# Conditioned attention with Strassen-Winograd products on one Trainium2 core: scale and shift formed for half of the channels at a time

## The chip, the cores and the metric

The kernel runs on one core of a Trainium2 (trn2) chip. The metric is the device time of one execution in microseconds (us), here the median of three executions.

## The reference

All arrays are float32. `x` is 4 x 1024 x 1024 (batch, token, channel), `cond` is 4 x 1024. Cut to what is computed:

```python
# attention part, 16 heads of 64
scale, shift = split(cond @ W_emb + b_emb, 2)          # W_emb: 1024 x 2048
xn  = rms_norm(x, g_norm) * (1 + scale) + shift        # per batch and channel
q, k, v = split(xn @ W_qkv)                            # W_qkv: 1024 x 3072
q, k = rms_norm(q, g_q), rms_norm(k, g_k)              # per head
o   = softmax(q k^T / 8) v
x   = x + o + o @ W_out
# depthwise causal convolution whose four taps are the four rows of cond
x   = x + conv(x, taps=cond) + b
```

No token can be multiplied with W_qkv before the scale and the shift of its channels are known, and these need a product with all of W_emb (8.4 MB).

## The kernel before

**The work.** For each batch and each of four pairs of head blocks (a `Double`, 16 in all, L530) the product `xn @ W_qkv` is made by Strassen and Winograd's scheme: tokens and channels are split in two, A11 being tokens 0 to 511 with channels 0 to 511, A12 the same tokens with channels 512 to 1023, A21 and A22 the later tokens. Seven products P1 to P7 of blocks or sums of blocks (S1 to S4 on the token side, T1 to T4 on the weight side) are made for four tiles of 128 tokens each: 28 pieces (`piece`, L580, matmuls at L589), each of four accumulated float32 matmuls over k = 0 to 3. P1 is A11 with the plain weights, P2 is A12 with the plain weights, P6 is S2 with T2, P7 is S3 with T3, P4 is A22 with T4, P5 is S1 with T1 and P3 is S4 with plain weights. A piece is evacuated from one of the three PSUM buffers of `ps_m` by ScalarE (P1, L599) or by VectorE (L601 to L610).

**Forming the sums.** `Chunk` (L257) makes, for one k and one half q of the token tiles, the blocks A and the sums S: four 128 x 128 transposes for the channel half c = 0 (`xtp`, L305), their evacuation with scale and shift (`modulate`, L250: ScalarE at L255, VectorE at L253), the same for c = 1, then four sums on VectorE (L321), and a store to the HBM scratch `scrA` (L329), from which later pieces load their operand `a` (L566). `direct` (L568) makes only A11 or A12 of the first tokens, without a trip through HBM (`xtd`, L574). `Weights` (L479) loads blocks of W_qkv (L495), forms T1 to T4 (L510, on GpSimd for the first Double, otherwise on VectorE) and stores them in `scrB` (L511); `load_w` (L540) fetches a piece's weights (plain ones at L547, T ones at L550, three buffers).

**The order.** The instruction order of all engines is written by hand: a planner's clock (`tick`) advances by the cost of each piece, steps are deferred by so many us of that clock, and `need` pulls a step forward. All loads and stores are issued in order by SyncE's queue (SP), which also waits there for the engines; the semaphores of its DMAs are used in turn, eight at a time, so a DMA waits for the eighth before it.

**The start of batch 0**, which the change rewrites, goes as follows.
1. Eight loads of W_emb for the scale (512 KB each, L369), then the first 512 tokens of x (eight loads of 256 KB, L351), then eight loads of W_emb for the shift. For each load two matmuls (L373) with the four columns of `condT` as the stationary operand and 512 columns of W_emb streaming; the result has four rows.
2. Each half is copied to SBUF (L149 by ScalarE, L151 by VectorE), sixteen small transposes (L380) bring scale and shift to the channel-per-partition layout, and L384 and L390 add bias and gain.
3. The weights of P1, the other 512 tokens (L344), the weights of P2, and the four `Weights` of the first Double are loaded. `direct(0, 0)` and `direct(1, 0)` make A11 and A12 of the first 256 tokens.
4. The loop over T runs the pieces in the order of FIRST_PRODUCTS (L521): P1 and P2 of tiles 0 and 1, P1 and P2 of tiles 2 and 3, then P6, P7, P4 for tiles 0, 1 and again for tiles 2, 3, then P5 and P3. Between the first of them stand the other two `direct` calls, the scaling of the second half of the tokens (squares at L222, scaling at L359) and the sixteen groups of chunk transposes.
5. The four `Weights` share two buffers of the tag `ob`; the third and the fourth load only after the first two are stored.

After the 28 pieces comes the loop over the 64 units (`Unit`, L618): scores (L629), softmax, values (L692), with the pieces of the next Doubles, the output products and the convolution put between them.

Of the kernel before, what the change touches and what calls it, by code (L numbers as in the profile page):

```python
# [10 lines left out]
F32 = mybir.dt.float32  # L11
AF = mybir.ActivationFunctionType
ALU = mybir.AluOpType
# [8 lines left out]
def kernel(  # L22
# [153 lines left out]
    nc.vector.tensor_copy(cols, cols_ps[:, :NR])  # L176

    condT = apool.tile([P, HN], F32, tag="rec", name="condT", bufs=1)
    condT = condT[:, : NJ * B].rearrange("p (j b) -> p j b", b=B)
    nc.vector.tensor_copy(condT, cols[:, R_COND:R_G].rearrange("p (b j) -> p j b", j=NJ))  # L180


    gqk = const.tile([P, 1], F32, name="gqk")
# [73 lines left out]
    class Chunk:  # L257
# [31 lines left out]
        def transposes(self, c):  # L289
            b, k, q = self.b, self.k, self.q  # L290
            need("xg", self.name)
            if c == 0:
                if len(combining) == 2:
                    d, *at = combining.pop(0)
                    need(*(("r", d, *at) if d else ("s", *at)))
                combining.append((b, q, k))
                tag, n, bufs = R_HOMES.get((q, k), R_HOME) if b == 0 else R_HOME
                rs = [
                    apool.tile([P, n, QN], F32, tag=tag, name=f"r_{self.name}_{i}", bufs=bufs) for i in range(0, 8, n)
                ]  # L300
                self.r = lambda i: rs[i // n][:, i % n, :]
                self.stores = [(rs[i // n][:, : min(n, 7 - i), :], i, min(i + n, 7)) for i in range(0, 7, n)]
            tp = ps_m.tile([P, 2, QN], F32, tag="m", name=f"xtp_{self.name}_{c}")
            for i in range(4):
                nc.tensor.transpose(tp[:, i // 2, i % 2 * P : (i % 2 + 1) * P], self.source(c, i), ident)  # L305
            tick(0.45)
            for h in range(2):
                place = ((A11, A21), (A12, A22))[c][h]
                modulate(self.r(place), tp[:, h, :], b, k + c * KH, b == 0 and c == 1)
            if c == 1:  # L310
                defer_quiet(1.2, ("s", q, k) if b == 0 else ("r", b, q, k), self.combine)

        def combine(self):
            r = self.r
            for place, (p0, p1, op) in {
                S1: (A21, A22, ALU.add),
                S2: (S1, A11, ALU.subtract),
                S3: (A11, A21, ALU.subtract),
                S4: (A12, S2, ALU.subtract),
            }.items():  # L320
                nc.vector.tensor_tensor(r(place), r(p0), r(p1), op)  # L321
            if (self.b, self.q) == (0, 0):
                defer(STORE, ("r", 0, 0, self.k), self.store)
            else:
                self.store()
# [3 lines left out]
                nc.sync.dma_start(scrA[self.b][self.q][:, i0:i1, self.k, :], src)  # L329


    mod_sb = []
    x0 = {}
    homes = [("qT00", 1), ("kT00", 1), ("qT01", 1), ("kT01", 1), ("v10", 2), ("v10", 2), ("v11", 2), ("v11", 2)]

    def first_tokens(h):
# [3 lines left out]
        for i, t in enumerate(tiles):  # L340
# [4 lines left out]
            else:  # L345
                x0[t] = []
                for g in range(2):
# [2 lines left out]
                    x0[t].append(xt)  # L350
                    nc.sync.dma_start(xt, x[0, t * P : (t + 1) * P, g * HN : (g + 1) * HN])  # L351

        def scale():
            for i, t in enumerate(tiles):
                norm.squares_of(i, x0[t])
            norm.root()
            for t in tiles:
                for g in range(2):
                    nc.vector.tensor_scalar_mul(x0[t][g], x0[t][g], rn[0, t])  # L359

        return scale

    for g in range(2):
        mod_ps = ps_s.tile([P, 2, HN], F32, tag="s", name=f"mod_ps_{g}")
        for k in range(NJ):
            if (g, k) == (1, 0):
                first_tokens(0)()
            we = apool.tile([P, 2, HN], F32, tag="sp", name=f"we_{g}_{k}", bufs=9)
            nc.sync.dma_start(  # L369
                we, w_emb[k * P : (k + 1) * P, g * DIM : (g + 1) * DIM].rearrange("p (h d) -> p h d", h=2)  # L370
            )
            for h in range(2):
                nc.tensor.matmul(  # L373
                    mod_ps[:B, h, :], condT[:, k, :], we[:, h, :], start=(k == 0), stop=(k == NJ - 1)
                )
        mod_sb.append(apool.tile([P, DIM], F32, tag=("mx", "sum")[g], name=f"mod_sb_{g}", bufs=1))
        evacuate(mod_sb[g][:B, :], mod_ps[:B].rearrange("p h d -> p (h d)"))
    modT_ps = ps_m.tile([P, 512], F32, tag="m", name="modT_ps")[:, : 2 * NJ * B]
    for c in range(2 * NJ):
        nc.tensor.transpose(  # L380
            modT_ps[:, c * B : (c + 1) * B], mod_sb[c // NJ][:B, c % NJ * P : (c % NJ + 1) * P], ident[:B, :B]
        )
    mod = const.tile([P, 2 * NJ, B], F32, name="mod")
    nc.vector.tensor_add(  # L384
        mod,
        modT_ps.rearrange("p (c b) -> p c b", b=B),
        cols[:, R_BE:R_GQ].unsqueeze(2).to_broadcast([P, 2 * NJ, B]),
    )
    gain = mod[:, :NJ, :]
    nc.vector.scalar_tensor_tensor(  # L390
        gain,
        mod[:, :NJ, :],
        1.0,
        cols[:, R_G:R_CB].unsqueeze(2).to_broadcast([P, NJ, B]),
        ALU.add,
        ALU.mult,
    )


    class Pair:  # L400
# [73 lines left out]
    def w_block(kh, c, k=None):  # L474

        rows = slice(kh * HN, (kh + 1) * HN) if k is None else slice(kh * HN + k * P, kh * HN + (k + 1) * P)
        return [w_qkv[rows, s * DIM + c * P : s * DIM + (c + 1) * P] for s in range(3)]

    class Weights:  # L479

# [5 lines left out]
        def load(self):  # L486
            d, k = self.d, self.k
            self.b = {}
            four = apool.tile([P, 4, HN], F32, tag="ob", name=f"b_{self.name}", bufs=2)
            for kh in range(2):  # L490
                for y in range(2):
                    t = four[:, 2 * kh + y, :]
                    self.b[kh, y] = t[:, :W3]
                    for s, src in enumerate(w_block(kh, 2 * d + y, k)):
                        nc.sync.dma_start(t[:, s * P : (s + 1) * P], src)  # L495
            if d:
                if d > 1 or k > 1:
                    defer_gap(5.0, ("B", d), 2.5, self.combine)
# [19 lines left out]
        PRODUCTS += [(name, a, t) for t in range(HT)]  # L518
    NPR = len(PRODUCTS)

    FIRST_PRODUCTS = PRODUCTS[:8]  # L521
    for ts in ((0, 1), (2, 3)):
        FIRST_PRODUCTS += [(name, a, t) for name, a in (("P6", S2), ("P7", S3), ("P4", A22)) for t in ts]
    FIRST_PRODUCTS += PRODUCTS[20:]
# [5 lines left out]
    class Double:  # L530
# [9 lines left out]
        def load_w(self, name):  # L540
# [2 lines left out]
            self.w[name] = w  # L543
            block = {"P1": (0, 2 * d), "P2": (1, 2 * d), "P3": (1, 2 * d + 1)}.get(name)
            if block:
                for s, src in enumerate(w_block(*block)):
                    nc.sync.dma_start(w[:, :, s * P : (s + 1) * P], src.rearrange("(k p) d -> p k d", p=P))  # L547
            else:
                need("B", d)
                nc.sync.dma_start(w, scrB[d][:, {"P6": T2, "P5": T1, "P7": T3, "P4": T4}[name]])  # L550
# [669 lines left out]
        return cut(pieces[:n], SHARES) + [pieces[n:]]  # L1220


    doubles[0] = Double(0)
    doubles[0].load_w("P1")
    scale = first_tokens(1)
    doubles[0].load_w("P2")
    for k in range(KH):
        weights[k] = Weights(0, k)
        weights[k].load()
    for s in range(2 * KH):  # L1230
        chunks[0, s] = Chunk(0, s % KH, s // KH)
    doubles[0].direct(0, 0)
    doubles[0].direct(1, 0)
    for k in range(KH):
        weights[k].combine()
    for T in range(NPR):
        if T in (1, 2):
            doubles[0].direct(T - 1, 1)
        if T == 1:
            scale()  # L1240
        if 2 <= T < 2 + KH:
            for s in range(2 * T - 4, 2 * T - 2):
                for c in range(2):
                    chunks[0, s].transposes(c)
        run(piece(T))

    own = []
# [85 lines left out]
```

## Time and profile before

| what | value |
|---|---|
| median of three executions | 2879.78 us (2879.61 to 2885.32) |
| the profiled execution: its own time | 2883.05 us |
| the profiled execution: its span | 2881.0 us |
| TensorE (PE) busy | 2790.8 us, 97% of the span |
| VectorE (DVE) / ScalarE (ACT) / GpSimd (POOL) busy | 76% / 58% / 47% |
| granted TensorE clock, mean | 0.991 |
| DMA | 510.98 MB, mean 177 GB/s |
| first piece (P1 of tile 0) begins | 42.24 us |
| first scores of the first unit begin | 146.20 us |

Times in the profile count from the start of the span. PEclk is the share of its full clock that TensorE was granted. A float32 matmul leaves two records, so a piece of four matmuls is "x8" in a timeline. "Idle before" is followed by what ended the idle time. DMA shares near 1.0 mean that the sixteen DMA engines had no spare time. SPq rows are DMA issues in SyncE's queue.

### The profile page before, as it was taken

The page shows a single profiled execution, that of the slowest core. Times are in us where ns is not written, and L with a number is a line of the kernel's source. Part 1 is how long each engine was busy: PE and PEld are TensorE (multiplying, and loading weights), DVE is VectorE, ACT ScalarE, POOL GpSimd, SP SyncE. Part 2 cuts the span into 40 slices and gives each one's busy share as a digit, 9 for nine tenths or more (in the row PEclk, how much of TensorE's full clock was granted, in tenths as well). Part 3 has the DMA queues.
Part 4 walks back from the last instruction along what each step waited for, and adds up shares of the span by engine and source line. Part 5 has one row for each costly group of instructions (what it writes and reads, how often), then busy time and mean ns, then how long its engine had stood idle before and what let it go on. Part 6 is the DMA issues. An engine that isn't in the chain of part 4 may idle for free.

```text
span 2881.0 us, 32179 instructions
## 1 busy us (share of the span) xinstructions
PE 2790.8 (97%) x10529; PEld 1315.6 (46%) x10529; DVE 2184.3 (76%) x2652; ACT 1684.7 (58%) x2269; POOL 1348.2 (47%) x534
## 2 busy tenths in 40 slices
PE   7999999999999999999999999999999999999999
PEld 3544444444444444544454444454444444444344
DVE  3578887888878776787878777778787868787863
ACT  3165757765556667765655667666565656555532
POOL 1045555555455543544544553454554455545520
PEclk9999999999999999999999999999999999999999
DMA  7864455755445646755655565665565445433433
GB/s 280 278 207 140 155 169 177 229 175 172 140 161 181 216 159 205 227 180 177 201 194 167 173 209 163 227 217 179 177 219 179 145 136 174 165 102 93 125 106 117
DMA packets 416254, 510.98 MB, mean 177 GB/s; under 512 B 41888, under 2 KB 327896, under 8 KB 406360
## 3 DMA queue, kind: packets, MB, share of 16 engines
q1 hardware_dynamic: 416088, 508.93, 54.2%
q8 instruction: 84, 1.38, 0.2%
q14 instruction: 82, 0.67, 0.1%
HBM read 413.43 MB, written 95.40 MB: 177 GB/s over the span
## 4 chain that ended last, share of the span: by engine, by line
PE 74%; DVE 12%; ACT 6%; DMA 4%; issue 3%; POOL 2%; SPq 1%; DVEq 0%; ACTq 0%; POOLq 0%
PE pqkv_P L589 28%; PE s L629 14%; PE pav L692 14%; PE po L950 5%; PE po_P L881 4%; DVE mx L646 4%; PE po L881 3%; DVE sp L665 2%; ACT sp L669 2%; ACT sp L637 1%; PE qkt L459 1%; PE tot L707 1%; DMA rec<-scrR 1%; DVE r L321 1%; DMA scrR<-few 1%
## 5 line engine op out<-in xcount | busy, mean ns | idle before, releaser
L589 PE MATMUL pqkv_P<-w_P,a 128*128 128x384 f32 x3504 | 1192.9, 491 | 27.7 <-issue 9.9
L671 POOL TENSOR_TENSOR sum<-sum,sp 128x1024 f32<-128x1024 f32 x384 | 958.9, 2497 | 64.7 <-ACT sp L669 34.2
L589 PEld LDWEIGHTS pqkv_P<-w_P,a 128*128 128x128 f32 x3504 | 649.8, 191 | 500.3 <-issue 85.8
L637 ACT COPY sp<-s 128x1024 f32<-128x1024 f32 x512 | 505.6, 1016 | 467.9 <-PE s L629 417.2
L646 DVE TENSOR_TENSOR mx<-mx,sp 128x1024 f32<-128x1024 f32 x384 | 515.4, 1342 | 158.2 <-ACT sp L637 131.3
L665 DVE TENSOR_TENSOR sp<-sp,mbp 128x1024 f32<-128x1024 f32 x512 | 604.6, 1212 | 18.5 <-ACT mbp L660 18.4
L669 ACT ACTIVATE sp<-sp 128x1024 f32<-128x1024 f32 x512 | 526.6, 1054 | 141.3 <-DVE sp L665 137.2
L651 POOL PARTITION_ALL_REDUCE mb<-mx x64 | 220.7, 3448 | 813.4 <-DVE mx L646 623.3
L629 PE MATMUL s<-qT,kT 64*128 64x512 f32 x2048 | 516.3, 620 | 19.5 <-DVE sp L665 12.4
L692 PE MATMUL pav<-sp,v 128*64 128x512 f32 x2048 | 487.0, 608 | 0.0
L671 POOL TENSOR_TENSOR sum<-sp,sp 128x1024 f32<-128x1024 f32 x64 | 151.3, 2364 | 489.1 <-ACT sp L669 258.7
L629 PEld LDWEIGHTS s<-qT,kT 64*128 64x128 f32 x2048 | 174.8, 186 | 311.1 <-issue 200.8
L986 DVE SCALAR_TENSOR_TENSOR y<-x,cols,y 128x512 f32<-128x512 f32 x192 | 248.9, 1301 | 48.3 <-ACT y L974 43.8
L692 PEld LDWEIGHTS pav<-sp,v 128*64 128x64 f32 x2048 | 131.4, 138 | 333.1 <-issue 323.2
L646 DVE TENSOR_TENSOR mx<-sp,sp 128x1024 f32<-128x1024 f32 x64 | 108.2, 1691 | 106.1 <-ACT sp L637 106.1
L608 DVE TENSOR_TENSOR qk<-u,pqkv_P 128x256 f32<-128x256 f32 x256 | 106.4, 416 | 82.5 <-PE pqkv_P L589 80.7
L950 PE MATMUL po<-ob,wo 128*128 128x512 f32 x352 | 155.1, 593 | 0.0
L881 PE MATMUL po_P<-o_P,wq_P 128*128 128x512 f32 x320 | 143.9, 592 | 0.0
L660 ACT COPY mbp<-mb 128x1024 f32<-128x1024 f32 x64 | 65.1, 1018 | 118.2 <-POOL mb L651 118.2
L451 DVE TENSOR_TENSOR qk<-qk,ms 128x1024 f32<-128x1024 f32 x64 | 125.9, 1968 | 2.2
L437 ACT ACTIVATE sq<-qk 128x512 f32<-128x512 f32 x128 | 76.9, 628 | 54.8 <-DVE qk L608 50.8
L881 PE MATMUL po<-o_P,wq_P 128*128 128x512 f32 x240 | 108.0, 592 | 0.0
(96 smaller groups left out, 1884.1 us busy)
## 6 DMA issues: line engine op xcount, KB each, us to landing
a<-scrA SPq DMA_DIRECT2D x215, 512.0 KB
w_P<-scrB SPq DMA_DIRECT2D x64, 768.0 KB
o_P<-scrS SPq DMA_DIRECT2D x40, 1024.0 KB
w_P<-in_L_cond_W_qkv_dram SPq DMA_DIRECT2D x144, 256.0 KB
o_P<-scrO SPq DMA_DIRECT2D x30, 1024.0 KB
scrA<-r SPq DMA_DIRECT2D x28, 896.0 KB
wq_P<-scrW SPq DMA_DIRECT2D x70, 256.0 KB
xc<-in_x_dram SPq DMA_DIRECT2D x64, 256.0 KB
```

Of the source, the lines that this page charges most:

```text
L589: nc.tensor.matmul(pm, (chunks[0, k].r(place) if a is None else a[:, k, :])[:, t % 2 * P : (t % 2 + 1) * P], w[:, k, :], start=(k == 0), s ...
L629: nc.tensor.matmul(ps[:, h, :], pr.kT[kt // HT][h * D : (h + 1) * D, kt % HT * P : (kt % HT + 1) * P], pr.qT[self.half][h * D : (h + 1) * ...
L637: nc.scalar.copy(sp, ps)
L646: nc.vector.tensor_max(self.mx, self.mx if kt > 1 else self.sp[0], self.sp[kt])
L651: nc.gpsimd.partition_all_reduce(self.mb.rearrange("p h q -> p (h q)"), self.mx.rearrange("p h q -> p (h q)"), P, bass_isa.ReduceOp.max,)
L665: nc.vector.tensor_sub(self.sp[kt], self.sp[kt], self.mb)
L669: nc.scalar.activation(sp, sp, AF.Exp)
L671: nc.gpsimd.tensor_tensor(self.sum, self.sum if kt > 1 else self.sp[0], sp, ALU.add)
L692: nc.tensor.matmul(self.pav[h * D : (h + 1) * D, :], self.pr.v[kt // HT][:, kt % HT, h * D : (h + 1) * D], self.sp[kt][:, h, :], start=(kt ...
L881: nc.tensor.matmul(pm, self.w[name][:, k, :], self.o[name][:, k, :], start=(k == 0 and name not in ("P2", "P3", "P4")), stop=(k == KH - 1),)
L950: nc.tensor.matmul(self.pm, self.w[kh][:, k % KH, :], oTs[b, k, half], start=False, stop=(k == NJ - 1),)
L986: nc.vector.scalar_tensor_tensor(self.y, self.x1[:, k : k + HN], cols[:, r : r + 1], self.y, ALU.mult, ALU.add)
```

## The change

- **The embedding by halves of the channels.** A class `Embed` handles 512 channels, scale and shift together. Its loads are sixteen of 256 KB (rows of 2 KB) instead of eight of 512 KB (rows of 4 KB). `condT` is padded with zeros to 32 columns; for each k four matmuls of 256 columns each write to the four groups of 32 output columns of the array (`ps[32 * g : 32 * (g + 1)]`), so the result stands in 128 rows by 256 columns. One copy (128 x 256, ScalarE), two 128 x 128 transposes and three small VectorE operations follow.
- **The order of the loads**: the first 512 tokens, W_emb of channel half 0, weights of P1, the other 512 tokens, W_emb of channel half 1, weights of P2, the four `Weights`.
- **The order of the pieces**: all four pieces of P1 (which need only half 0) stand before the second half's embedding, then the four of P2. `across(c, q)` makes the chunk transposes of one channel half for all four k; c = 0 of q = 0 stands before the first piece of P2, c = 1 of q = 0 after it; c = 0 of q = 1 stands before the first piece of P6 and c = 1 after it.
- **Chunks, in all batches**: S3 = A11 - A21 is formed after the c = 0 transposes, the other three sums after c = 1.
- **`Weights`**: one load for three column blocks (192 KB) instead of three of 64 KB, in all Doubles that load them; for the first Double the third and the fourth `Weights` get buffers of their own (tags `oT`, `ou2`, `ou4`, `x`).
- **Plain weights in `load_w`**, in all 16 Doubles (P1, P2, P3: 48 loads): four DMAs of 192 KB, one for each k, instead of three of 256 KB.

From the first piece of P6 on, the built TensorE order is the same in both kernels but for the four groups of c = 1 transposes behind it. The diff, cut to its core:

```diff
-    condT = condT[:, : NJ * B].rearrange("p (j b) -> p j b", b=B)
+    condT = condT[:, : NJ * 32].rearrange("p (j b) -> p j b", b=32)
+    nc.vector.memset(condT, 0.0)
...
-            if c == 1:
-                defer_quiet(1.2, ("s", q, k) if b == 0 else ("r", b, q, k), self.combine)
+            key = ("s", q, k) if b == 0 else ("r", b, q, k)
+            if c == 0:
+                defer_quiet(1.2, key, lambda: self.sums({S3: (A11, A21, ALU.subtract)}))
+            else:
+                defer_quiet(1.2, key, self.combine)
...
+    class Embed:
...
+            rooms = [("sp", 9)] * 8 if half == 0 else [("sp", 9), ("mx", 1), ("sum", 1)] + [("qk", 3)] * 3
...
+        def load(self):
+            for k, w in enumerate(self.w):
+                for g in range(2):
+                    at = g * DIM + self.half * HN
+                    nc.sync.dma_start(w[g], w_emb[k * P : (k + 1) * P, at : at + HN])
+
+        def run(self):
+            half = self.half
+            ps = ps_m.tile([P, 512], F32, tag="m", name=f"mod_ps_{half}")[:, :QN]
+            for k in range(NJ):
+                for g in range(4):
+                    nc.tensor.matmul(
+                        ps[32 * g : 32 * (g + 1), :],
+                        condT[:, k, :],
+                        self.w[k][g // 2][:, g % 2 * QN : (g % 2 + 1) * QN],
+                        start=(k == 0),
+                        stop=(k == NJ - 1),
+                    )
+            sb = apool.tile([P, HN], F32, tag="xs", name=f"mod_sb_{half}", bufs=2)[:, :QN]
+            nc.scalar.copy(sb, ps)
+            mt = ps_m.tile([P, 512], F32, tag="m", name=f"modT_ps_{half}")[:, :QN]
...
+            for i in range(2):
+                nc.tensor.transpose(mt[:, i].rearrange("p g b -> p (g b)"), sb[:, i * P : (i + 1) * P], ident)
...
-        return [w_qkv[rows, s * DIM + c * P : s * DIM + (c + 1) * P] for s in range(3)]
+        return w_qkv.rearrange("r (s c) -> r s c", s=3)[rows, :, c * P : (c + 1) * P]
+
+    W_HOMES = {(0, 2): [("oT", 2)] * 2 + [("ou2", 1), ("ou4", 1)], (0, 3): [("x", 6)] * 4}
...
-    FIRST_PRODUCTS = PRODUCTS[:8]
+    FIRST_PRODUCTS = [PRODUCTS[i] for i in (0, 1, 4, 5, 2, 3, 6, 7)]
...
-                for s, src in enumerate(w_block(*block)):
-                    nc.sync.dma_start(w[:, :, s * P : (s + 1) * P], src.rearrange("(k p) d -> p k d", p=P))
+                for k in range(KH):
+                    nc.sync.dma_start(w[:, k], src[:, k])
...
+    squares_0(range(HT))
+    scale_0()
+    embeds[0].run()
+    first.direct(0, 0)
+    first.direct(0, 1)
     for k in range(KH):
         weights[k].combine()
+    START = {
+        1: [lambda: squares_1(range(2))],
+        2: [lambda: squares_1(range(2, HT)), scale_1],
+        4: [embeds[1].run, lambda: first.direct(1, 0), lambda: across(0, 0)],
+        5: [lambda: first.direct(1, 1), lambda: across(1, 0)],
+        8: [lambda: across(0, 1)],
+        9: [lambda: across(1, 1)],
+    }
     for T in range(NPR):
-        if T in (1, 2):
-            doubles[0].direct(T - 1, 1)
-        if T == 1:
-            scale()
-        if 2 <= T < 2 + KH:
-            for s in range(2 * T - 4, 2 * T - 2):
-                for c in range(2):
-                    chunks[0, s].transposes(c)
+        for step in START.get(T, ()):
+            step()
         run(piece(T))
```

## Prediction

> **What bounds the kernel now.** I read the page's busy shares first (PE 97% of the span), then the stretches of 10 us for the first 160 us, then PE's timeline there. After 150 us the list of PE's waits holds some 60 us in 2730, of them 1.5 on a DMA; so TensorE is the bound from there on, and its order there is untouched. The place where time lies about is the start.
>
> ```profile
> core 0: us, PE busy (x) PEld busy (x) DVE busy (x) ACT busy (x) POOL busy (x), PEclk, DMA share, GB/s
> 10.00:20.00 10.00, 10.00 (x22) 1.92 (x21) 0.00 (x0) 0.00 (x0) 0.00 (x0) 1.00 1.03 413
> 30.00:40.00 10.00, 9.28 (x40) 3.15 (x38) 5.07 (x12) 1.04 (x2) 0.00 (x0) 1.00 1.06 390
> 40.00:50.00 10.00, 8.78 (x41) 5.29 (x39) 3.18 (x6) 7.01 (x18) 4.95 (x5) 1.00 0.63 177
> 50.00:60.00 10.00, 5.30 (x21) 3.84 (x22) 7.32 (x15) 5.13 (x14) 4.10 (x5) 0.66 0.65 216
> 60.00:70.00 10.00, 7.33 (x28) 4.58 (x28) 9.59 (x20) 2.18 (x5) 3.42 (x4) 0.84 0.65 203
> 70.00:80.00 10.00, 8.76 (x48) 6.07 (x47) 9.53 (x24) 4.45 (x9) 4.04 (x4) 0.99 0.64 227
> 80.00:90.00 10.00, 10.00 (x33) 5.81 (x32) 5.68 (x15) 1.95 (x4) 0.00 (x0) 1.00 1.06 332
> ```
>
> To 40 us the DMA engines are full (share above 1) and PE is busy with nothing but the embedding; from 40 to 80 us the DMA is at 0.64 while PE, VectorE and ScalarE wait in turn.
>
> ```profile
> start us, us, engine line op out<-in xcount [idle before <-releaser]
> 7.16 30.33 PE L373 MATMUL mod_ps<-we,condT 128*4 128x512 f32 x64 [2.32 <-DMA we<-in_L_cond_W_emb_dram]
> ...
> 42.24 2.79 PE L589 MATMUL pqkv_P<-w_P,a 128*128 128x384 f32 x8
> ...
> 52.48 1.07 PE L574 MATMUL xtd<-ident,x 128*128 128x128 f32 x4 [2.96 <-ACT u L599]
> ...
> 87.39 5.32 PE L589 MATMUL pqkv_P<-w_P,r 128*128 128x384 f32 x16
> 96.14 12.25 PE L589 MATMUL pqkv_P<-w_P,r 128*128 128x384 f32 x32 [3.43 <-DMA w_P<-scrB]
> 108.23 10.48 PE L589 MATMUL pqkv_P<-w_P,a 128*128 128x384 f32 x32
> ...
> 146.20 1.99 PE L629 MATMUL s<-qT,kT 64*128 64x512 f32 x8
> ```
>
> Embedding to 37.5 us, first piece at 42.24, then scattered idle spells, a wait for scratch weights until 96.14, and from 108.23 (P6 of tile 2) to the first scores at 146.20 a dense 38.0 us. From that piece on nothing in PE's order changes, so the question is when P6 of tile 2 starts. A piece takes 2.58 us (5.16 for the sixteen records at 124.58, from their start to the next start).
>
> ```profile
> 192.24 0.64 PE L707 MATMUL tot<-sum,ones 128*32 128x256 f32 x8
> 192.81 1.99 PE L629 MATMUL s<-qT,kT 64*128 64x512 f32 x8
> ```
>
> This is the only operation before that has the form of the new embedding: four matmuls, 32 output columns each, 256 streamed columns. All four take 0.57 us to the next start, while one matmul of 512 columns in the embedding takes 13.91/16 = 0.87.
>
> **The change part by part.**
>
> *First piece.* DMA moved 1.6 MB by 10 us, then 0.418 MB/us. Now 2.1 MB of x and 4.2 MB of W_emb come first: 10 + 4.7/0.418 = 21.2 us, landed by 21.8. (A DMA alone needs some 2.4 us besides its bytes, an estimate from the first W_emb load: issued at 3.46, matmul at 7.16, 1.25 of it for 0.52 MB. In a full queue only the end of this shows.) Squares (8 x 0.61, paced by the loads), table load 1.28, scaling 3.26 for eight end near 18.6, hidden by the W_emb loads; so are the memset of condT and the seven first k of matmuls. On the path: the last k 0.6, a copy of 128 x 256 0.38 (L725), two transposes 0.4, three small VectorE operations 0.6 (L384, L390), and the eight tiles of `direct`, which took 2.5 from L390's end to the first piece. Sum 4.5: the first piece at 26.3 instead of 42.24. P1's weights land near 24.
>
> *P1, then the second half.* Four pieces are 10.3 us. Here the Trainium skill speaks against the change ("TensorE: Matmul & The Clock Gate", Part 1): after an idle window of some 3.4 us the array runs at half clock until it has been busy as long, which makes, as an estimate, 1.7 lost each time. The rows agree in kind and are dearer: PEclk falls to 0.66 in the stretch with the idle 2.96, and the four pieces after the 3.43 us idle took 12.25, against 10.48 for the next four (1.8 more). Before, the long embedding kept PE busy; now it runs in short spells between loads. I take 1.9 at P1, 1.3 behind the second half and 1.0 later, 4.2 in all (the rule: 5.1; nothing if PE stays warm). P1 ends at 26.3 + 12.2 = 38.5. Its ScalarE copies and the second squares fit below it. Meanwhile 0.8, 2.1 and 4.2 MB land by 38.8 to 39.3, so W_emb's second half arrives just as PE comes free: 8 x 0.57 = 4.6, copy, transposes and VectorE 1.5: half 1 known at 44.6. These matmuls are a new wait in PE's queue: if the loads are late, every piece behind them is late by as much, and the cover is thin, 0 to 1 us.
>
> *Chunks.* ScalarE now evacuates ten 256-column tiles (two of `direct`, eight of `across`) at 0.51 in sequence: 44.6 to 49.7, and P2's first piece needs the buffer freed 2 us earlier: 47.6 to 50.2. `across(1, 0)` alternates ScalarE and VectorE; VectorE has six evacuations at 0.5 and three sums ahead of the last one, sums at 0.77 while GpSimd forms T (4.62 for six): P2's second piece at 54, three pieces 7.7 and 1.3 cold: 63. VectorE's nine later sums lie below these. Then eight ScalarE evacuations, two squares of 0.63, so P6 can start near 67.
>
> *P6's weights.* The rule of the skill's "DMA: Bandwidth & Descriptors" (Rules for kernel authors: at least 1 MiB per DMA) speaks against the 256 KB W_emb loads. By its fit of 2.0 us + bytes/436 GB/s, one 256 KB load alone runs at 100 GB/s, and 24 of them would take 62 us; but x came in such loads between 10 and 18 us at 402 to 422 GB/s, eight in flight. I take the row. For 64 KB loads rule and row agree:
>
> ```profile
> 36.45 13.58 SPq L495 DMA_DIRECT2D b<-in_L_cond_W_qkv_dram x24
> ```
>
> Twenty-four of 64 KB took 13.58 us (116 GB/s). As 192 KB loads (512 B rows, 0.27 to 0.34 MB/us when full) the four `Weights` arrive between 43 and 52 us, since two no longer wait for the others' stores. Then GpSimd bounds: 16 x 1.04 = 16.6, from 43.3 to 60; the last T2 is formed near 59, its store lands near 61; the load of 0.79 MB, issued at 61.5, lands near 65.5 (2.3 at 0.35 and a DMA's fixed part). The borrowed `x` buffers, which chunk k = 1 of q = 1 takes next, come free near 62, before its evacuation near 64: 0, or 2 if GpSimd is slower. That is under the 67 above, against 87.39 before. P7's and P4's buffers are free since P1 and P2 are done, so the 3.43 us wait goes.
>
> *P6 to P4, then the a-tiles.* Six pieces 15.5, the c = 1 transposes of q = 1 behind the first of them 3.3, cold 1.0: 67 + 19.8 = 86.8. P6 of tile 2 needs the stores of all chunks with q = 1, made near 77: from 61 us the DMA has 2.4 MB of weights, 1.4 MB of q = 0 stores, 3.7 MB of q = 1 stores and 0.6 MB of the next weights, 8.1 MB at 0.35 = 23 us, so 84, and the load 3: 87 to 88. I take 88. First scores 88 + 38.0 = 126 instead of 146.2: 20.2 us gained.
>
> *The repeated edits.* S3 ahead of its siblings (24 chunks in batches 1 to 3): VectorE's built order changes by next to nothing and the sums are the same; 0. One DMA issue more in each of 48 weight loads (0.46 on SP) is covered by loads that are issued pieces ahead (no PE wait for w_P after 146 us but where SP itself stood behind stores); eight fewer issues in each of twelve `Weights`. 0, between -3 and +3.
>
> Sum against the profiled execution: 2883.05 - 20.2 = 2862.9. It lies 3.3 above the median, which I subtract: 2859.6, or 2860.
>
> **The rivals.**
> - *Column groups don't overlap.* If four products of 256 columns run one after another, a half costs 32 x 0.435 = 13.9 us instead of 4.6: 4.6 more before the first piece (it was half hidden by loads) and, the queue behind it being short, 9.3 less that spare of about 1 and the cold time that vanishes, in the second: first scores near 138, gain 8, 2872. Against: 0.57 us for four in the row above.
> - *The DMA takes the wait.* The same bytes in 20 us less. If stores and loads run at 0.27 (as 512 B rows do at full share, or as 239 to 266 GB/s between 70 and 82 us) instead of 0.35, the 8.1 MB need 30 us: P6 of tile 2 at 94 to 95, scores at 132.5, gain 13.5: 2866. Against: 352 to 365 GB/s between 86 and 94 us with the same mixture.
> - *Slower: VectorE stands behind ScalarE in every later chunk.* S3, called after c = 0, waits for two evacuations (0.51 each) on ScalarE, which may lie behind score copies or exponentials of 1.02 to 1.05 us each; VectorE's shifts and evacuations queue behind S3, and PE behind those. At 2.1 us in each of 24 chunks it costs 50, net 30 slower: 2910. It decides from (20.2 + 5.8)/24 = 1.1 us a chunk. Against: in the built order S3 is followed at once by sums that wait for later ScalarE work anyway.
> - *Dense PE.* No cold time and no wait for a-tiles: P6 of tile 2 at 82, gain 26: 2854.
>
> **How the numbers follow.** My case with its spread (2854 to 2865, the dense case being its edge) 0.72; the DMA case 0.13; the serial groups 0.10; slower 0.04; nothing measurable (the gain given back in later units) 0.01. Likeliest 2860. The range takes in the dense case less 3 for the repeated edits and all but the edge of the serial case: 2851 to 2871. Within 0.2% (5.8 us), which a measurement of this kernel can hardly tell from no change: 0.02; slower by more 0.04; faster 0.94.
>
> **What would show it.** Right: first piece near 26 us, four matmuls of the embedding in about 0.6 us, second half known near 45, P6's first piece near 67, P6 of tile 2 near 88, first scores near 126, and equal lengths from there to the end. Wrong: DMA share below 0.9 before 40 us; embedding matmuls that start 0.2 us apart; P6's first piece waiting for scrB long after 67; a wait for `a` of over 4 us at P6 of tile 2; or more PE idle in front of scores after the start, with VectorE behind ScalarE's `r`.

## The result and the profile after

| | before | after |
|---|---|---|
| median of six executions each, run side by side | 2882.04 us | 2871.81 us (2868.63 to 2876.04) |
| ratio after/before, 95% interval | | 0.9963 [0.9951, 0.9976] |
| the profiled execution: its own time / its span | 2883.05 / 2881.0 us | 2868.63 / 2866.9 us |
| first piece (P1 of tile 0) begins | 42.24 us | 27.10 us |
| P6 of tile 0 / P6 of tile 2 begins | 87.39 / 108.23 us | 70.75 / 95.86 us |
| first scores begin | 146.20 us | 136.82 us |
| from the first scores to the end of the span | 2734.8 us | 2730.1 us |

The kernel became faster by 10.2 us, half of the forecast 20.2, and the median lies 0.8 us above the range. The profiled execution of after is the fastest of its six, 3.2 us under their median, so 5 of the 14.4 us between the two profiled executions are no part of the start. In the start the gain is 9.4 us where 20.2 were forecast.

The timeline of TensorE in after, to be held against the one of before:

```profile
start us, us, engine line op out<-in xcount [idle before <-releaser]
...
27.10 10.54 PE L643 MATMUL pqkv_P<-w_P,a 128*128 128x384 f32 x32
37.57 4.64 PE L404 MATMUL mod_ps<-we,condT 128*32 128x256 f32 x64
...
54.55 8.01 PE L643 MATMUL pqkv_P<-w_P,a 128*128 128x384 f32 x24
65.62 2.39 PE L307 MATMUL xtp<-ident,x 128*128 128x128 f32 x16 [3.06 <-DVE v L662]
70.75 4.51 PE L643 MATMUL pqkv_P<-w_P,r 128*128 128x384 f32 x8 [2.74 <-DMA w_P<-scrB]
...
77.43 13.20 PE L643 MATMUL pqkv_P<-w_P,r 128*128 128x384 f32 x40
95.86 13.47 PE L643 MATMUL pqkv_P<-w_P,a 128*128 128x384 f32 x32 [5.23 <-DMA a<-scrA]
...
136.82 1.99 PE L683 MATMUL s<-qT,kT 64*128 64x512 f32 x8
```

To P2's end at 62.56 all goes as forecast: the first piece 15.1 us earlier, four dense pieces of P1, and 64 small matmuls in 4.64 us. Then three waits stand where none or a short one was expected: for VectorE (3.06), for P6's weights (2.74) and for the `a` tile of P6 of tile 2 (5.23). The last two are followed by slow products: 4.51 us for a first piece, 13.47 for four pieces that took 10.48 before (PEclk is 0.75 from 90 to 100 us); the sixteen transposes behind the first are not slow (2.39 us).

The stretches of 10 us, as shown of before:

```profile
core 0: us, PE busy (x) PEld busy (x) DVE busy (x) ACT busy (x) POOL busy (x), PEclk, DMA share, GB/s
...
40.00:50.00 10.00, 8.67 (x59) 5.08 (x52) 5.19 (x9) 5.15 (x11) 4.62 (x5) 1.00 1.05 311
50.00:60.00 10.00, 8.75 (x42) 5.71 (x41) 8.90 (x15) 3.28 (x6) 9.45 (x10) 1.00 0.91 313
60.00:70.00 10.00, 4.90 (x24) 2.82 (x23) 7.47 (x16) 3.71 (x8) 2.80 (x3) 1.00 0.76 258
```

From 40 to 60 us the DMA moves 311 to 313 GB/s at a share near 1, where before had 177 to 216 at 0.63 to 0.65. From 60 to 70 us neither the DMA nor any engine is busy for more than 0.76 of the time: here the engines wait for each other.

Two more views say on what. SyncE's queue, whose rows are DMA issues, and VectorE:

```profile
39.63 11.38 SPq L546 DMA_DIRECT2D b<-in_L_cond_W_qkv_dram  x16
51.11 12.20 SPq L562 DMA_DIRECT2D scrB<-b  x16
...
64.09 2.31 SPq L604 DMA_DIRECT2D w_P<-scrB  x3
66.51 18.76 SPq L338 DMA_DIRECT2D scrA<-r  x10
...
90.50 1.29 SPq L620 DMA_DIRECT2D a<-scrA  x3
```

```profile
57.94 7.01 DVE L321 TENSOR_TENSOR r<-r 128x256 f32<-128x256 f32 x9
64.87 0.41 DVE L662 TENSOR_TENSOR qk<-u,pqkv_P 128x256 f32<-128x256 f32 x1
65.20 0.28 DVE L662 TENSOR_TENSOR v<-u,pqkv_P 128x128 f32<-128x128 f32 x1
```

Ten stores of chunks, the last seven of them q = 1's, are issued over 18.76 us: of these the queue waits 7.6 at one stretch for ScalarE's evacuation behind the c = 1 transposes and 5.4 for VectorE, whose last sum ends at 84.7. The `a` loads follow at 90.50, when the last of these stores has landed, and the first lands at 95.7. In VectorE nine sums stand ahead of P2's evacuation (L662), so P2's PSUM buffers come free only from 65.5 on.

### The profile page after: what moved, and what is told of

Its sections match the earlier page's. It is cut to its first block, busy times and chain, and to the rows that moved or that the text cites. A ratio compares the mean times of both kernels' runs of the same rounds, so it can differ in the third digit from the quotient of the medians.

```text
span 2866.9 us, 32127 instructions
## 1 busy us (share of the span) xinstructions
PE 2766.6 (97%) x10581; PEld 1310.3 (46%) x10581; DVE 2183.8 (76%) x2648; ACT 1689.7 (59%) x2278; POOL 1347.7 (47%) x534
## 4 chain that ended last, share of the span: by engine, by line
PE 72%; DVE 13%; DMA 5%; ACT 4%; issue 3%; POOL 2%; SPq 1%; DVEq 0%; ACTq 0%; POOLq 0%
PE pqkv_P L643 28%; PE s L683 14%; PE pav L746 14%; PE po L1004 5%; PE po_P L935 4%; DVE mx L700 4%; PE po L935 3%; DVE sp L719 3%; DVE r L321 1%; POOL sum L725 1%; ACT sp L691 1%; PE qkt L502 1%; PE tot L761 1%; ACT sp L723 1%; DMA rec<-scrR 1%
## 5 line engine op out<-in xcount | busy, mean ns | idle before, releaser
L683 PE MATMUL s<-qT,kT 64*128 64x512 f32 x2048 | 514.1, 618 | 20.0 <-DVE sp L719 12.8
L662 DVE TENSOR_TENSOR qk<-u,pqkv_P 128x256 f32<-128x256 f32 x256 | 106.0, 414 | 78.3 <-PE pqkv_P L643 76.9
```

The costliest lines, as they stand in the source:

```text
L683: nc.tensor.matmul(ps[:, h, :], pr.kT[kt // HT][h * D : (h + 1) * D, kt % HT * P : (kt % HT + 1) * P], pr.qT[self.half][h * D : (h + 1) * ...
```

## The experiments

Theory A: the missing half went to a chain of waits in the start, in which the c = 1 transposes behind P6's first piece, VectorE's sums and the stores in SyncE's queue follow each other. Rival B: the DMA's bytes set when P6's weights and the `a` tile land, whatever the order. A second question is which part of the change the gain belongs to.

Each ratio is to runs of the kernel before made beside it. The medians of those runs lie between 2881.05 and 2884.77 us, so rows are to be compared by their ratios rather than by their medians. "Rest" is the profile's time from the first scores to the end of the span.

| kernel | P6 of tile 0, of tile 2 | first scores | rest | median us | ratio [95%] |
|---|---|---|---|---|---|
| before | 87.39, 108.23 | 146.20 | 2734.8 | | 1 |
| after | 70.75, 95.86 | 136.82 | 2730.1 | 2871.81 | 0.9963 [0.9951, 0.9976] |
| e1 | 74.49, 92.58 | 130.62 | 2732.2 | 2867.44 | 0.9943 [0.9931, 0.9956] |
| e2 | 68.50, 94.09 | 135.07 | 2736.4 | 2872.55 | 0.9964 [0.9955, 0.9973] |
| e3 | 71.53, 95.87 | 136.82 | 2739.0 | 2873.48 | 0.9968 [0.9956, 0.998] |
| e4 | 72.60, 90.33 | 128.38 | 2736.6 | 2866.44 | 0.9942 [0.9928, 0.9955] |
| e5 | 69.66, 92.16 | 131.89 | 2737.9 | 2875.24 | 0.9966 [0.9956, 0.9976] |
| e6 | 65.64, 89.90 | 130.95 | 2735.5 | 2870.74 | 0.995 [0.9935, 0.9965] |
| e7 | 84.65, 100.17 | 138.14 | 2742.8 | 2883.54 | 0.999 [0.998, 1.0] |
| e8 | 80.50, 105.37 | 146.31 | 2738.0 | 2882.1 | 0.9995 [0.9984, 1.0005] |
| e9 (after again) | 70.37, 96.75 | 136.48 | 2734.1 | 2873.01 | 0.9971 [0.9958, 0.9985] |
| e10 (e7 again) | 85.47, 101.70 | 139.67 | 2741.7 | 2882.45 | 0.9991 [0.9981, 1.0002] |
| e11 | 84.99, 100.47 | 138.44 | 2733.9 | 2876.56 | 0.9985 [0.9977, 0.9992] |
| e12 | 70.65, 95.96 | 137.01 | 2730.4 | 2875.94 | 0.9974 [0.9964, 0.9983] |
| e13 | 70.51, 95.10 | 136.03 | 2735.0 | 2869.47 | 0.9956 [0.9943, 0.9968] |
| e14 | 73.38, 92.44 | 132.01 | 2730.8 | 2864.55 | 0.994 [0.9926, 0.9953] |

**e1: the c = 1 transposes in front of P6's first piece.**

```diff
-        8: [lambda: across(0, 1)],
-        9: [lambda: across(1, 1)],
+        8: [lambda: across(0, 1), lambda: across(1, 1)],
```

> The c = 1 transposes of q = 1 stand in front of P6's first piece instead of behind it, all else as in the changed kernel. Theory A (a chain: the first P6 piece waits for the T weights, the q = 1 transposes stand behind it on PE, VectorE's last sums and their store and load follow): the transposes fit into the idle time before 70.75 us, P6's first piece stays near 71, the last q = 1 sum ends near 77 instead of 84.7, the a-tile lands near 89, P6 of tile 2 begins near 89.5 instead of 95.9, first scores near 129, time about 8 us below the changed kernel. Theory B (DMA bytes alone: all that is moved between 64 and 96 us): the a-tile lands no more than 1 to 3 us earlier, first scores near 134, time 1 to 4 us below.

TensorE's timeline of e1:

```profile
67.03 2.86 PE L307 MATMUL xtp<-ident,x 128*128 128x128 f32 x16 [3.06 <-DVE v L662]
...
74.49 16.02 PE L643 MATMUL pqkv_P<-w_P,r 128*128 128x384 f32 x48
92.58 10.56 PE L643 MATMUL pqkv_P<-w_P,a 128*128 128x384 f32 x32 [2.06 <-DMA a<-scrA]
```

P6 of tile 0 begins 3.7 us later than in after, and P6 of tile 2 still 3.3 us earlier: VectorE's last sum ends at 80.6 instead of 84.7, and the `a` loads are issued at 88.09 instead of 90.50. With a wait of 2.06 instead of 5.23 us the four pieces keep the clock (10.56, not 13.47). First scores come 6.2 us earlier, and the ratio falls from 0.9963 to 0.9943: moving one group of transposes recovers more than half of the 10.8 us that the start misses. Theory A had asked for more (P6 still near 71, scores near 129) and B for less (134).

In e1 the planner also moved 1.4 MB of q = 0's stores, which in after stand ahead of the `a` load, behind it. The DMA in after, stretch by stretch, tells what these bytes cost:

```profile
core 0: us, PE busy (x) PEld busy (x) DVE busy (x) ACT busy (x) POOL busy (x), PEclk, DMA share, GB/s
79.00:80.00 1.00, 1.00 (x4) 0.57 (x3) 0.97 (x3) 0.00 (x0) 0.00 (x0) 1.00 0.00 1
80.00:95.70 15.70, 10.63 (x33) 5.81 (x31) 7.11 (x18) 0.00 (x0) 0.00 (x0) 0.97 0.95 322
```

From 79 to 80 us the DMA stands still: its next store was issued at 79.08, after 1.5 us of waiting for VectorE. What was issued before had landed by then and did not delay q = 1's larger stores. From 80 us to the landing the DMA is nearly full with those stores and the loads behind them. An earlier last sum alone, with the same bytes behind it, was not tried, so no run shows how these last 15.7 us divide between the sums and the bytes.

**e4: e1, with q = 0's stores due earlier.**

```diff
-    STORE = 30.0
+    STORE = 20.0
```

> As the first of these runs (transposes in front of P6), but the stores of the q = 0 chunks are due 10 us of planner's clock earlier, so that one chunk's stores (0.9 MB) are issued ahead of the first a-tile's load. Theory A: the last sum is as early as there (77), the a-tile lands 1 to 3 us later than there (92 or less), first scores near 131. Theory B: each 0.9 MB ahead of the a-tile costs 2.7 us, first scores 2.7 later than there, whatever the sums do.

With 0.9 MB more of q = 0's stores ahead of the `a` load, the scores begin 86.1 us after the second half's transposes (42.24), against 86.5 (44.12) in e1, where B asked for 2.7 us more. But three loads of the next `Weights` (0.6 MB), ahead of the `a` load in e1, stand behind it here, so that only 0.3 MB were added: this run hardly tests B. What speaks against B as the only cause is the standstill after 79 us.

**e2: the first Double's T sums left out; e5: only T2 stored; e6: both.** In e2 GpSimd forms nothing for the first Double. In e5 the stores of T1, T3 and T4 are left out, and P5, P7 and P4 of the first Double use T2 instead.

```diff
-                (nc.vector if self.d else nc.gpsimd).tensor_tensor(dst, p0, p1, ALU.subtract)
+                if self.d:
+                    nc.vector.tensor_tensor(dst, p0, p1, ALU.subtract)
```

```diff
-                nc.sync.dma_start(scrB[self.d][:, place, self.k, :], dst)
+                if self.d or place == T2:
+                    nc.sync.dma_start(scrB[self.d][:, place, self.k, :], dst)
...
-                nc.sync.dma_start(w, scrB[d][:, {"P6": T2, "P5": T1, "P7": T3, "P4": T4}[name]])
+                nc.sync.dma_start(w, scrB[d][:, {"P6": T2, "P5": T1, "P7": T3, "P4": T4}[name] if d else T2])
```

> The sums T of the first Double are left out (its weight blocks are stored as they were loaded), so GpSimd does nothing in the start; all else as in the changed kernel. Theory A with contention (GpSimd's sums slow VectorE's and both hold up P2's evacuation and P6's weights): VectorE's q = 0 sums take 0.42 us instead of 0.8 to 1.2, the 3.06 us wait at 62.6 us is gone, P6's first piece begins near 66 instead of 70.75, first scores near 131, time about 5 us below the changed kernel. Without contention: sums stay at 0.8 or more, the wait before P6 shrinks only by the weights' part, first scores near 134. Theory B: the a-tile lands at 93 or later, first scores near 134.

> The changed kernel, but for the first Double only the T2 blocks are stored, and P7, P4 and P5 of that Double load T2 in place of T3, T4 and T1 (so its products are not the reference's); GpSimd's sums stay. 2.4 MB less are written ahead of P6's weights. If GpSimd's sums (to 62.9 us) hold P6: the last T2 is stored near 62, P6's weights land near 68, first P6 piece near 69 instead of 70.75, first scores 1 to 2 us earlier. If DMA bytes alone hold it: P6's first piece near 66 (bounded by the transposes before it), the a-tile 5 to 7 us earlier, first scores near 131.

> As the run before, and GpSimd's T sums are left out as well. With both the sums and 2.4 MB of stores gone, P6's weights should land by 60 to 61 us if the two together were what held them (they landed at 68.4 without the sums and at 70.6 with both), and P6's first piece begins when the c = 0 transposes of q = 1 are done, near 64.5; first scores near 129 to 131, since the q = 1 transposes still stand behind that piece. If something else holds the weights, P6's first piece stays near 68.

VectorE in e2 (the same sums as at 57.94 in after), then TensorE in e2:

```profile
56.07 3.84 DVE L321 TENSOR_TENSOR r<-r 128x256 f32<-128x256 f32 x9
59.83 0.41 DVE L663 TENSOR_TENSOR qk<-u,pqkv_P 128x256 f32<-128x256 f32 x1
```

```profile
68.50 4.90 PE L644 MATMUL pqkv_P<-w_P,r 128*128 128x384 f32 x8 [4.25 <-DMA w_P<-scrB]
```

Without GpSimd nine sums take 3.84 instead of 7.01 us, P2's evacuation begins 5.0 us earlier and the wait of 3.06 is gone. Yet P6 begins only 2.3 us earlier, since its weights land at 68.5: the DMA is at a share of 0.99 to 1.01 from 50 to 70 us (338 GB/s) with loads and stores. With the sums kept and three quarters of the stores left out (e5) it begins at 69.66, 3.06 for VectorE and 0.97 for its weights; with both gone (e6) at 65.64, held there by ScalarE and no longer by its weights. The load of these weights is issued at 64.09 in after, at 62.48 in e2 behind the stores, at 63.38 in e5 behind GpSimd, and at 58.58 in e6. So two paths end almost together here, GpSimd's sums and the bytes of the stores: taking one away brings 1 to 2 us, both together 5. From issue to P6's first piece it is 6.7 us in after and still 6.0 and 6.3 in e2 and e5; in all of them a chunk's store (0.9 MB) is issued just ahead and the weights of two more pieces (1.5 MB) just behind. In all three the wait for `a` is again 4.3 to 6.1 us. The first scores of e5 and e6 begin 4.9 and 5.9 us earlier than after's; by their ratios (0.9966, 0.995) e5 gains nothing over after and e6 some 3 us, so part of it is given back behind the start.

**e7 and e10: the merged loads alone, on the kernel before.**

```diff
-        return [w_qkv[rows, s * DIM + c * P : s * DIM + (c + 1) * P] for s in range(3)]
+        return w_qkv.rearrange("r (s c) -> r s c", s=3)[rows, :, c * P : (c + 1) * P]
...
-                    for s, src in enumerate(w_block(kh, 2 * d + y, k)):
-                        nc.sync.dma_start(t[:, s * P : (s + 1) * P], src)
+                    nc.sync.dma_start(t[:, :W3].rearrange("p (s c) -> p s c", s=3), w_block(kh, 2 * d + y, k))
...
+                for k in range(KH):
+                    nc.sync.dma_start(w[:, k], src[:, k])
```

> The kernel before with the merged weight loads alone (192 KB instead of 64 KB; plain weights in four DMAs), nothing else of the change. If the merged loads are a source of the gain: the first Weights' 24 loads take 6 us instead of 13.6, first scores 2 to 5 us before 146.2. If the gain comes from the order of embedding and pieces: first scores within 2 us of 146.2 (the wait at 92.7 us is for weights whose buffer comes free at 82 us), time within 2 us of the kernel before.

> The kernel before with the merged loads alone, profiled once more: its first scores came 8.1 us earlier than before's, yet its time was hardly shorter, since the stretch behind the first scores was 8 us longer. If that stretch is only the draw of one profile, it comes out near 2735 now and the time near 2876; if the earlier start itself is given back later, first scores come again at 138 within 1 us, the stretch is again above 2739, and the time stays within 0.2 per cent of before's.

**e8: the order alone**, that is after with those three edits taken back; **e9: after, unchanged.**

> The changed kernel with its loads of weights as they were before (three transfers for each block of Weights and for each plain weight, 112 in the place of 32 and so on), all the rest of the change kept: halves, column groups, order of the products, split of the sums. With this the four corners of order and loads are there. Theory A (two effects that overlap: both shorten the same start, whose end is set by the chain embedding, P2, P6, and by the arrival of the weights): the merged loads alone brought the first scores forward by 8.1 us, both together by 9.4, so the order alone brings little once Weights' loads are late again: first scores at 137 to 143, a time within 5 us of the changed kernel, above it. Theory B (the order alone carries the gain, and the merged loads cost or bring nothing beside it): first scores within 1 us of 136.8 and the time within 2 us of the changed kernel's. A ratio above 0.999 would say that the gain needs both.

> The changed kernel, unchanged, profiled once more beside its corners. If what lies ahead of the first scores is decided by order and transfers, these begin again at 136.8 within 1 us, and the stretch behind them (2730.1 in the first profile) comes out between 2730 and 2738: the variation of a time lies behind the first scores, where waits of some 2 us are followed by slow products in one profile and not in another.

SyncE's queue in e8, a stretch of e8 (the last two figures are DMA share and GB/s), TensorE in e8, and TensorE in e7:

```profile
39.37 25.34 SPq L547 DMA_DIRECT2D b<-in_L_cond_W_qkv_dram  x48
64.82 7.86 SPq L563 DMA_DIRECT2D scrB<-b  x16
```

```profile
50.00:65.00 15.00, 11.70 (x50) 7.07 (x48) 13.76 (x21) 3.27 (x6) 10.90 (x11) 1.00 0.48 130
```

```profile
80.50 4.50 PE L642 MATMUL pqkv_P<-w_P,r 128*128 128x384 f32 x8 [11.41 <-DMA w_P<-scrB]
...
105.37 13.45 PE L642 MATMUL pqkv_P<-w_P,a 128*128 128x384 f32 x32 [5.01 <-DMA a<-scrA]
```

```profile
84.65 15.69 PE L590 MATMUL pqkv_P<-w_P,r 128*128 128x384 f32 x48
100.17 10.48 PE L590 MATMUL pqkv_P<-w_P,a 128*128 128x384 f32 x32
```

This is the study's main reading. In e8 the first piece begins at 28.23, 14 us earlier than before, and P2 ends at 62.2; but the 48 small loads take SyncE 25.34 us (3.1 MB, so 0.12 MB/us, with the DMA at a share of 0.48 from 50 to 65 us), P6 waits 11.41 us, and the first scores begin at 146.31, where before had them at 146.20. The order alone brings nothing. In e7 the order is the old one, P6 of tile 0 begins only 2.7 us earlier than before, but next to nothing waits after it, and the scores begin at 138.14. So in the start the merged loads alone bring 6.5 to 8.1 (e7, e10) of the 9.4 to 9.7 us (after, e9), and the order adds 1 to 3 us only beside them.

Neither theory of e8 held: its scores came later than A's 137 to 143, and its time lay 9 us above that of e9, where A asked for less than 5. The third sign, a ratio above 0.999, did come: by it the gain in time needs both. In time e7 and e10 gain only 1 to 3 us where their scores begin 8.1 and 6.5 earlier; the rest is 2742.8 and 2741.7, 7 to 8 us longer than before's, in both profiles. So most of that start is given back later, and not by the draw of one profile. Part of it hangs on the later Doubles' loads: e11, below, has the merged loads in the first Double's plain weights and in the `Weights` alone, and its ratio is 0.9985 [0.9977, 0.9992], a gain of 4 us.

**e3, e11, e12, e13: the repeated edits.** Undone are, in the later Doubles only, the plain weights in four transfers (e3, e11, e13), and in batches 1 to 3 the split of the sums (e3, e12); e11 stands on e7, the others on after.

```diff
-                for k in range(KH):
+                for k in range(KH) if self.n == 0 else ():
                     nc.sync.dma_start(w[:, k], src[:, k])
+                for s in range(3) if self.n else ():
+                    nc.sync.dma_start(w[:, :, s], src[:, :, s])
```

```diff
-            if c == 0:
+            if c == 0 and b == 0:
...
-            else:
+            elif c == 1:
...
                     S2: (S1, A11, ALU.subtract),
+                    **({S3: (A11, A21, ALU.subtract)} if self.b else {}),
```

> The changed kernel with its repeated edits undone: S3 formed with its siblings in batches 1 to 3, and the plain weights loaded in three DMAs in all Doubles but the first. The start is as in the changed kernel (first scores near 136.8). If the repeated edits cost or gain nothing: time within 2 us of the changed kernel. If they cost the missing 10 us: time 10 us below it.

> The kernel before with the loads of Weights merged and the plain weights of the first Double alone in four transfers; the plain weights of the 15 later Doubles go in three transfers, as in before. Beside it stands the run with all loads merged, whose first scores came 6.5 to 8.1 us earlier than before's and whose time was 1 to 2 us shorter, so that some 6 us were given back behind the first scores. Theory A (the 45 later plain weights in four transfers, P1, P2 and P3 of 15 Doubles, cost that: more transfers in a queue that everything shares): the first scores stay at 138 to 140 and the time falls to 2875 to 2878. Theory B (the earlier start itself is given back, by waits behind it that depend on where the loads of the next piece stand): the time stays at 2881 to 2884.

> The changed kernel with the split of the sums undone in batches 1 to 3 alone (S3 formed with the other three sums again); the plain weights stay in four transfers everywhere. With both repeated edits undone the time had not moved (2873.48 beside 2871.81 and 2873.01). Theory A (two repeated edits that cancel: the later transfers cost some 6 us, the split brings as much, since VectorE's waits in front of the second head's scores fall from 2.5 us to some 1 to 2 and the 16 products after them keep the full clock): 2877 to 2880. Theory B (both at nothing): 2871 to 2875.

> The changed kernel with the 45 plain weights of the 15 later Doubles in three transfers again; the split of the sums is kept in all batches. It is the fourth corner of the two repeated edits, beside the changed kernel (four transfers, split: 2871.81 and 2873.01, ratios 0.9963 and 0.9971), split undone (four transfers: 2875.94, 0.9974) and both undone (2873.48, 0.9968). Theory A (the four transfers cost some 5 us behind the first scores, the split brings as much): 2866 to 2869, ratio near 0.995. Theory B (neither does anything that can be measured): 2871 to 2875, ratio 0.996 to 0.9975. First scores at 136.8 by both.

By the ratios, four transfers against three: 0.999 and 0.9991 against 0.9985 on the old order, 0.9963 and 0.9971 against 0.9956 on after, 0.9974 against 0.9968 with the split undone. Split kept against undone: 0.9963 and 0.9971 against 0.9974, 0.9956 against 0.9968. All five comparisons have the sign of theory A (the later transfers cost, the split brings as much), at 1.5 to 3.5 us, a quarter to two thirds of what it asked for. No pair's intervals are apart, so the cancelling is likely and not shown. e11's own forecast of 2875 to 2878 came true, but its runs of before lay 3 us under those of e7; e12 and e13 fell between the two theories. With both repeated edits out of the way, the merged loads alone bring 4 us (e11, 0.9985) and the order another 5 beside them (e3, 0.9968).

TensorE near 635 us, first in after, then in e7, shows the kind of place where the rest differs:

```profile
633.57 1.13 PE L683 MATMUL s<-qT,kT 64*128 64x512 f32 x4 [1.14 <-DVE sp L719]
634.63 3.65 PE L746 MATMUL pav<-sp,v 128*64 128x512 f32 x16
```

```profile
639.48 1.13 PE L630 MATMUL s<-qT,kT 64*128 64x512 f32 x4 [2.46 <-DVE sp L666]
640.54 5.35 PE L693 MATMUL pav<-sp,v 128*64 128x512 f32 x16
```

The wait for VectorE is 1.3 us longer, and the 16 products behind it take 1.7 us more. In the rest of after TensorE waits nine times in this way, 12.8 us in all, beside other waits of the same size, and each may or may not cost the second amount.

**e14: e1 with the later plain weights in three transfers.**

> The version with all transposes of the second half of the chunks in front of the first piece of P6 (2867.44, ratio 0.9943), and the plain weights of later Doubles in three transfers as well. Theory A of the repeated edits: 2861 to 2864, ratio near 0.9925. Theory B: 2866 to 2868, ratio 0.994 to 0.9945. First scores near 130.6 by both.

2864.55 us, 2.9 under e1 and the lowest median of all, but at 0.994 its ratio is e1's; its scores began at 132.01, since the four pieces of P6 and P7 of tiles 2 and 3 were slow (12.08). So it decides for theory B in the ratio and lies between the two in time. e1, e4 and e14 agree within their intervals and lie below both kernels of the case; their intervals still touch after's first (from 0.9951) but not its second (e9, from 0.9958).

## Why the prediction was wrong

- *First piece, P1, second half: right.* 27.10 for 26.3; the second half's matmuls 4.64 for 4.6 and half 1 known near 44; P2's first piece 47.21 for 47.6; P2 ends at 62.56 for 63. The column groups overlap, so the first rival is out. One term was too dear: no time is lost to a cold array at P1 (10.54 for four pieces, where 1.9 were added) or behind the second half. The loss came where I had put least.
- *"VectorE's nine later sums lie below these": failed.* Their size was right (9 x 0.77 = 6.9; 7.01 measured), their place was not. They end at 64.87, behind P2's last piece, and P2's evacuation queues behind them; TensorE waits 3.06 us for PSUM. Without GpSimd's sums (e2) they take 3.84 us and the wait is gone.
- *P6's weights at 65.5: failed by 5.2 us* (70.7). I bounded the step by GpSimd. It began 1.8 later and took 17.9 instead of 16.6, so the load was issued at 64.09 instead of 61.5; and it took 6.6 us to land, not 4.0, beside a chunk's store and the weights of the next two pieces. e2 and e5 show that the bytes of the T stores, to which I gave no room, hold the issue nearly as long as GpSimd does, and that the 6 us of landing stay without either. P6's first piece: 70.75 for 67.
- *P6 of tile 2 at 88: failed by 7.9 us*, the largest term. I took the c = 1 transposes as 3.3 us of TensorE and bounded the `a` tile by bytes (8.1 MB at 0.35). But the sums of q = 1 stand behind these transposes, which stand behind P6's first piece: the last is made at 84.7, not 77, then its store, the loads at 90.50, and 5.2 us to land. The step that failed is thus "made near 77", and with it the count of bytes from 61 us, which took the DMA as fed without a break. Of the 7.7 us, 3.8 are P6's late start, 1.8 its slow first piece (4.35 us to the next start for 2.58) and 3 VectorE, which took 7.1 us from the last transpose (77.6) to the last sum where my sum left 4; the transposes themselves were 1 us shorter. e1 moves the transposes and takes 3.3 of the 7.9 us at this point although P6 itself begins later. The DMA rival named the wait and its time (94 to 95; 95.86), but not its rate of 0.27: the DMA moved 0.315 MB/us from 61 to 90.5 us (9.3 MB, not 8.1) and 0.322 from 80 us on, and stood idle behind VectorE after 79. What stays open is how much an earlier last sum would bring against the bytes behind it.
- *The 38.0 us from there to the first scores: 41.0.* The 5.23 us wait costs a second time, 3.0 us of slow products in the four pieces behind it. 7.9 and 3.0 make the 10.8 us between 126 and 136.8.
- *Repeated edits 0 ± 3: right as a sum* (0.9968 with both undone, 0.9963 and 0.9971 with both), perhaps as two terms of 1.5 to 3.5 us of opposite sign, which would be luck.
- *Slower by VectorE behind ScalarE: did not happen*; with the split kept the times are, if anything, shorter.
- *"For 64 KB loads rule and row agree": in direction alone.* The fit of that page of the Trainium skill ("DMA: Bandwidth & Descriptors", Anatomy of one DMA) is stated for DMAs issued from GpSimd; for one load of 64 KB alone it gives, as an estimate, 30 GB/s, and the row shows 116 with several in flight. The forecast rests on the row.

## What to carry to other kernels

When a producer is moved forward, walk every queue between it and the next fixed point, and ask of each step which instruction stands behind which: the largest miss was a place in a queue, and so was the one at VectorE; most durations were right, a load's landing and VectorE's last sums were not. Price a wait of TensorE with what it does to the products behind it. And test the parts alone: here the order without the merged loads brings nothing that stands clear of noise (0.9995), and by the ratios the merged loads without the order bring 3 to 4 us (e7, e10, e11) and both together 8 to 11 (after, e9).

## What the runs showed of the hardware

- A sum of two 128 x 256 float32 blocks on VectorE (L321) takes 0.42 us, and up to 1.23 while GpSimd forms T; in e2, without GpSimd's sums, none takes above 0.43. That the two share an interface to SBUF when VectorE reads two inputs there is stated by the Trainium skill ("GPSIMD Engine Reference", section 1, Specifications); the price is from these rows.
- The same 3.1 MB of `Weights` took SyncE's queue 25.34 us as 48 loads of 64 KB (e8; 0.53 each, the DMA share at 0.48) and 11.38 as 16 of 192 KB (after; the share near 1).
- At two places (near 635 and near 708 us, the second half of a head's scores waiting for VectorE), in the 16 profiles, 15 waits of 0.9 to 1.9 us left the 16 products behind them at full clock (3.65 us) every time; of 17 waits of 2.1 to 3.5 us, 13 were followed by 4.3 to 5.7 us and 4 were not. At other places waits of 1.75 us (before, at 404) and 1.83 us (e9, at 242) were followed by 4.78 and 5.35 us, so 1.9 is no threshold. The Trainium skill ("TensorE: Matmul & The Clock Gate", Part 1) lets the clock fall only after an idle window of some 3.4 us and counts the windows freely, whatever the program does. The price that follows from it as an estimate, half the clock for one window or 1.7 us, fits these rows (5.35 - 3.65), though after 5.23 us idle it was 3.0 (13.47 - 10.48); its threshold does not, for waits of 1.8 to 2.2 us already paid it; windows that run freely would explain why equal waits do not pay alike, which no run here shows.
- Such slow products may be much of the difference between executions: in the rest of e3 TensorE is busy for 2669.7 us, in that of after for 2657.9, with the same matmuls, and the rests differ by 8.9.
